# Transposing the next image in pairs of rows over four cycles, and averaging channel groups on VectorE by block transposes

## Chip, cores and metric

The kernel runs on one core of one Trainium2 chip. The time is that of one execution on the device, in microseconds (us), as the median of several executions. TensorE is the matmul engine (PE in the profile, PEld its weight loads), VectorE is DVE, ScalarE is ACT, GpSimd is POOL. L262 is line 262 of the kernel that is being spoken of.

## The reference

A batch of 32 images of 56 x 56 pixels and 128 channels, fp32, goes through two layers. Each is `x + layer(group_norm(x))` with 32 groups of 4 channels.

```python
# layer 0: shifted-window attention, 7 x 7 windows, 4 heads
x = x + attention(group_norm(x))
# layer 1: cosine transforms over width and over height, 32 modes mixed
# per mode by a 128 x 128 matrix, inverse transforms, then 128 -> 512 -> 128
x = x + feedforward(fourier(group_norm(x)))

def group_norm(v, G=32, eps=1e-5):          # v: B, H, W, C
    g = v.reshape(B, H, W, G, C // G)
    m, s = g.mean((1, 2, 4)), g.var((1, 2, 4))
    return (g - m) / sqrt(s + eps)
```

## The kernel before

An image is eight rows of windows. The kernel works in cycles, one per row: each cycle does the attention of one row of this image, in three stages on three rows, and a slice of the Fourier layer of the two images before. Behind an image's eighth cycle comes the first row of the next image, which must be ready by then: its pixels are transposed to channels on partitions (`image_group`), its statistics are gathered (`bn_stats`), and its group averages turn into the scale and shift of the first norm (`image_norm`). A generator's `yield` is where the cycle goes on with other work: `next(norm)` is called once behind the keys, once ahead of the second feed-forward matmul, and once at the cycle's end.

```python
    def image_group(im, i):                      # row i of windows: 3.5 tiles of 112 pixels
        pt = attn_bank()
        pt4 = pt[:, : 8 * S].rearrange("p (j r s) -> p j r s", r=8, s=WS)
        for c in range(4):                       # so every other tile is transposed twice
            nc.tensor.transpose(pt4[:, :, 2 * c : 2 * c + 2], im.x[:, WS * i // 2 + c], ...)
        mine = pt4[:, :, i % 2 : i % 2 + WS].rearrange("p j r s -> p j (r s)")
        ...
        nc.scalar.copy(xw.rearrange("p (j t) -> p j t", t=WT), mine)
        nc.vector.bn_stats(im.st[:, i], xw)
        ...
        nc.gpsimd.tensor_tensor(piece, piece, bproj..., ALU.add)     # the projection's bias

    def image_norm(im):
        mv = small.tile([P, 2], F32, tag="mv", name="mv")
        nc.vector.bn_aggr(mv, im.st)
        yield
        pg = attn_bank()                         # group mean: a block-diagonal matrix of 1/4
        nc.tensor.matmul(pg[:, 0:1], lhsT=gavg, rhs=mv[:, 0:1], start=True, stop=True)
        ...                                      # gm = mean; e = (mean_c - gm)^2 + var_c
        yield
        pv = attn_bank()                         # group variance
        nc.tensor.matmul(pv[:, 0:1], lhsT=gavg, rhs=e, start=True, stop=True)
        ...
        nc.gpsimd.tensor_tensor(rstd, ve, mhalf, ALU.pow)
        nc.vector.scalar_tensor_tensor(out=nb, in0=gm, scalar=-1.0, in1=rstd, ...)
        yield
        nc.scalar.mul(im.w, wqkv, rstd)
        pb = attn_bank()
        nc.tensor.matmul(pb[:, 0:1], lhsT=wqkv[:, 2 * C :], rhs=nb, start=True, stop=True)
        ...
    # in the cycle:
            for j in {4: (0, 1), 5: (2, 3, 4), 6: (5, 6, 7)}.get(i, ()):
                image_group(images[b + 1], j)
```

There is one `k_sb` and one `q_sb`; the keys are written twice, once by ScalarE and once by VectorE:

```python
    def attn_max(r):
        nc.vector.tensor_reduce(mx, a3, axis=AX.X, op=ALU.max)
        nc.gpsimd.tensor_tensor(a3, a3, mx..., ALU.subtract)
    def attn_exp(r):
        nc.scalar.activation(a3, a3, AF.Exp)
    def attn_qk(im, i, first):
        ...                                      # matmul into pq; ScalarE -> q
        ...                                      # matmul into pk; ScalarE -> k_sb[:, 0]
            nc.vector.tensor_scalar(k_sb[:, 1], pk3, ...)
    def full_last(cycle, norm):
        next(norm)
        ...                                      # second feed-forward matmul
        next_image(cycle)                        # transposes of the next image
        attn_exp(cycle)                          # ahead of the next cycle's keys
        attn_project(im, j)
        next(norm)
```

## Time and profile before

| | before |
|---|---|
| time, first 3 runs | 3686.11 us (3684.14 to 3687.61) |
| TensorE busy | 99% of the span, 61440 matmuls |
| VectorE, ScalarE, GpSimd busy | 59%, 58%, 37% |
| distance between the width transforms of two images, smallest of 29 | 112.51 us |
| the same, mean of 29 | 112.72 us |

The last two rows are the measure. They are read from TensorE's timeline: the start of one image's width cosine transform (L597, 112 matmuls) to the start of the next image's. All 32 images do the same work between those points, so the smallest distance is an image without irregular stops (I call it the floor) and the mean is what the time is made of. The first and last distances are left out, since they touch the start and the end.

### The profile page before, as it was taken

How to read it: one execution, taken by the hardware profiler on the slowest of the kernel's cores; microseconds unless marked ns; L12 is line 12 of the kernel's file. 1: busy time of each engine (PE TensorE's matmuls, PEld its weight loads, DVE VectorE, ACT ScalarE, POOL GpSimd, SP SyncE). 2: the span in 40 equal slices, each digit the busy share in tenths (PEclk: the TensorE clock that was granted, in tenths of full speed). 3: DMA queues.
4: the chain of work that ended last, by engine and by line, in shares of the span. 5: the costliest groups of instructions: out<-in, count | busy, mean ns of one | idle time of the engine just before them, and what ended most of it. 6: DMA issues, size and time to landing. Idle time of an engine off the chain costs nothing.

```text
span 3682.2 us, 139931 instructions
## 1 busy us (share of the span) xinstructions
PE 3627.3 (99%) x61440; PEld 2964.9 (81%) x61440; DVE 2184.9 (59%) x4580; ACT 2146.4 (58%) x3915; POOL 1370.7 (37%) x1421
## 2 busy tenths in 40 slices
PE   7899999999999999999999999999999999999999
PEld 5788888888888888888888888878888888888877
DVE  7656666556666556665566656566655566655641
ACT  5565555655556655566556565555565565665553
POOL 5333334333434333433334343334343333433321
PEclk9999999999999999999999999999999999999999
DMA  4334433433433334334334334343334343443333
GB/s 115 97 101 111 108 105 96 118 106 102 116 96 107 107 106 113 101 101 115 106 102 115 96 109 108 106 113 97 105 107 111 101 114 96 114 108 105 97 106 92
DMA packets 687792, 388.91 MB, mean 106 GB/s; under 512 B 40495, under 2 KB 658128, under 8 KB 686928
## 3 DMA queue, kind: packets, MB, share of 16 engines
q1 hardware_dynamic: 686573, 379.65, 37.7%
q8 instruction: 483, 7.91, 0.9%
q14 instruction: 125, 1.02, 0.1%
q10 hardware_dynamic: 611, 0.32, 0.0%
HBM read 218.29 MB, written 161.48 MB: 103 GB/s over the span
## 4 chain that ended last, share of the span: by engine, by line
PE 93%; DVE 4%; ACT 1%; DMA 1%; issue 0%; SPq 0%; POOL 0%; ACTq 0%; DVEq 0%; POOLq 0%
PE pc L733 20%; PE pc L713 18%; PE pa L355 7%; PE pc L631 6%; PE pc L597 6%; PE pa L377 5%; PE pa L421 5%; PE pa L488 5%; PE pa L330 5%; PE pc L670 5%; PE pa L446 4%; PE pa L323 4%; PE pa L261 2%; DVE a L385 1%; DVE st L272 1%; DVE mx L395 1%
## 5 line engine op out<-in xcount | busy, mean ns | idle before, releaser
L410 POOL TENSOR_TENSOR a<-a,rs 128x784 f32<-128x784 f32 x256 | 389.4, 1521 | 1218.7 <-DVE rs L409 958.7
L733 PE MATMUL pc<-wff,hid 128*128 128x128 f32 (+1 forms) x6400 | 778.8, 279 | 1.0 <-ACT hid L721 0.8
L733 PEld LDWEIGHTS pc<-wff,hid 128*128 128x128 f32 (+1 forms) x6400 | 731.4, 190 | 22.1 <-issue 2.9
L713 PE MATMUL pc<-xf,wff 128*128 128x512 f32 (+2 forms) x1792 | 713.4, 541 | 1.3 <-DVE xf L681 0.6
L721 ACT ACTIVATE hid<-pc,b1sb 128x512 f32<-128x512 f32 (+2 forms) x896 | 536.0, 635 | 93.3 <-PE pc L713 89.5
L713 PEld LDWEIGHTS pc<-xf,wff 128*128 128x128 f32 x1792 | 337.0, 190 | 302.6 <-issue 228.8
L396 POOL TENSOR_TENSOR a<-a,mx 128x784 f32<-128x784 f32 x256 | 389.2, 1520 | 462.3 <-DVE mx L395 451.1
L745 DVE TENSOR_TENSOR res<-pc,res 128x512 f32<-128x512 f32 (+3 forms) x259 | 143.8, 566 | 599.8 <-issue 282.0
L429 ACT COPY aT<-pa 113x452 f32<-113x452 f32 x256 | 137.3, 537 | 453.6 <-PE pa L421 453.5
L276 POOL TENSOR_TENSOR xl<-xl,bproj 112x384 f32<-112x384 f32 (+1 forms) x256 | 291.5, 1140 | 244.4 <-PE pa L261 240.3
L385 DVE TENSOR_TENSOR a<-pa,bm 128x392 f32<-128x392 f32 x512 | 259.7, 550 | 203.1 <-PE pa L377 202.9
L343 DVE TENSOR_SCALAR k<-pa,heads,bqkv 128x392 f32<-128x392 f32 x246 | 168.6, 685 | 279.3 <-ACT k L335 279.3
L402 ACT ACTIVATE a<-a 128x784 f32<-128x784 f32 x256 | 223.0, 871 | 182.6 <-POOL a L396 180.3
L477 DVE TENSOR_SCALAR oT<-pa,bqkv 128x98 f32<-128x98 f32 (+2 forms) x768 | 171.0, 279 | 259.3 <-PE pa L446 259.3
L362 ACT COPY v<-pa 128x512 f32<-128x512 f32 x256 | 152.5, 596 | 267.8 <-PE pa L355 267.6
L703 POOL TENSOR_TENSOR res<-res,b2sb 128x512 f32<-128x512 f32 (+2 forms) x256 | 263.2, 1034 | 96.2 <-DMA res<-scr 86.1
L377 PEld LDWEIGHTS pa<-k,q 64*64 64x64 f32 x8192 | 183.4, 132 | 128.3 <-DVE rs L409 68.2
L355 PE MATMUL pa<-wn,xw 128*64 128x128 f32 x4096 | 282.3, 280 | 3.6 <-DVE a L385 2.8
L355 PEld LDWEIGHTS pa<-wn,xw 128*64 128x64 f32 x4096 | 220.2, 137 | 53.5 <-issue 17.5
L395 DVE TENSOR_REDUCE mx<-a 128x16 f32<-128x784 f32 x256 | 247.4, 966 | 5.5
L421 PE MATMUL pa<-ident,a 113*113 113x113 f32 x2048 | 248.7, 265 | 0.9 <-POOL a L410 0.9
L407 DVE TENSOR_REDUCE sm<-a 128x16 f32<-128x784 f32 x256 | 245.9, 960 | 5.1 <-ACT a L402 5.1
(89 smaller groups left out, 5888.8 us busy)
## 6 DMA issues: line engine op xcount, KB each, us to landing
zscr<-z SPq DMA_DIRECT2D x512, 112.0 KB
htok<-scr SPq DMA_DIRECT2D x256, 196.0 KB
zT<-zscr SPq DMA_DIRECT2D x192, 256.0 KB
res<-scr SPq DMA_DIRECT2D x160, 256.0 KB
out_dram<-res SPq DMA_DIRECT2D x128, 256.0 KB
scr<-xl SPq DMA_DIRECT2D x128, 224.0 KB
xl<-in_x_dram SPq DMA_DIRECT2D x32, 784.0 KB
xl<-in_x_dram SPq DMA_DIRECT2D x32, 672.0 KB
```

What stands on the lines that cost most here:

```text
L276: nc.gpsimd.tensor_tensor(piece, piece, bproj.unsqueeze(1).to_broadcast([TC, n1 - n0, C]), ALU.add)
L355: nc.tensor.matmul(pv[hs, j * C : (j + 1) * C], lhsT=im.xw[i][:, w * WT : w * WT + JP], rhs=im.w[:, 2 * C : 3 * C], start=True, stop=True,)
L377: nc.tensor.matmul(ps[hp][HALVES[e], pr * 2 * WT : (pr + 1) * 2 * WT], lhsT=q[cs, w * WT : w * WT + JP], rhs=k_sb[cs, :, w], start=True, s ...
L385: nc.vector.tensor_tensor(a[:, 2 * hp : 2 * hp + 2, :, 0:WT].rearrange("p u w j -> p w u j"), ps[hp][:, :RT].rearrange("p (w u j) -> p w u ...
L395: nc.vector.tensor_reduce(mx, a3, axis=AX.X, op=ALU.max)
L396: nc.gpsimd.tensor_tensor(a3, a3, mx.unsqueeze(2).to_broadcast([P, 2 * NWR, WT]), ALU.subtract)
L410: nc.gpsimd.tensor_tensor(a3, a3, rs.unsqueeze(2).to_broadcast([P, 2 * NWR, WT]), ALU.mult)
L421: nc.tensor.transpose(pt[:PW, h * P : h * P + PW], a[:PW, h, 2 * hf : 2 * hf + 2].rearrange("p w j -> p (w j)")[:, :PW], ident[:PW, :PW],)
L703: nc.gpsimd.tensor_tensor(res[:m, c0:c1], res[:m, c0:c1], b2sb[:m].unsqueeze(1).to_broadcast([m, c1 - c0, C]), ALU.add,)
L713: nc.tensor.matmul(ph[:, :n], lhsT=wff1[:, f * P : (f + 1) * P], rhs=xff[:, t0 : t0 + n], start=True, stop=True,)
L721: nc.scalar.activation(hf[:, :n], ph[:, :n], AF.Relu, bias=b1sb[:, f : f + 1])
L733: nc.tensor.matmul(pf[:m, c * C : (c + 1) * C], lhsT=im.hid[f][:, c * P : c * P + m], rhs=wff2[:, f], start=(f == 0), stop=(f == NF - 1),)
```

## The change

The intent is to take matmuls from the engine that bounds the kernel. Two rows of windows are 7 whole tiles, so a pair needs 7 transposes where two single rows need 8; four pairs are spread over the fourth to seventh cycles. The two averaging matmul pairs go: VectorE transposes the 128 x 32 statistics within 32 x 32 blocks, so that a group of four channels lies along the free axis, reduces there, and transposes back. That chain stands behind the keys of the eighth cycle.

```diff
-    def image_group(im, i):
-        pt = attn_bank()
-        for c in range(4):
+    def image_groups(im, i):
+        pt = [attn_bank(), attn_bank()]
+        for c in range(7):
             nc.tensor.transpose(...)
-        nc.scalar.copy(xw.rearrange("p (j t) -> p j t", t=WT), mine)
-        nc.vector.bn_stats(im.st[:, i], xw)
+        for k in range(2):
+            ...                          # one copy for row 0, a small and a large one for row 1
+            nc.vector.bn_stats(im.st[:, i + k], xw)
...
     def image_norm(im):
-        nc.vector.bn_aggr(mv, im.st)
         yield
-        pg = attn_bank()
-        nc.tensor.matmul(pg[:, 0:1], lhsT=gavg, rhs=mv[:, 0:1], start=True, stop=True)
...
-        yield
-        pv = attn_bank()
-        nc.tensor.matmul(pv[:, 0:1], lhsT=gavg, rhs=e, start=True, stop=True)
+        nc.vector.bn_aggr(stat[:, 0:2], im.st)
+        nc.vector.transpose(turned, stat)
+        average(mean[:, 0], turned)      # tensor_reduce, then tensor_scalar by 0.25
+        nc.vector.tensor_tensor(turned, turned, mean[:, 0], ALU.subtract)
+        nc.vector.tensor_tensor(turned, turned, turned, ALU.mult)
+        average(mean[:, 1], turned)
+        nc.vector.transpose(back..., mean...)
...
         nc.gpsimd.tensor_tensor(rstd, ve, mhalf, ALU.pow)
+        yield
         nc.vector.scalar_tensor_tensor(out=nb, in0=gm, scalar=-1.0, in1=rstd, ...)
+        nc.scalar.mul(im.w, wqkv, rstd)
         yield
-        nc.scalar.mul(im.w, wqkv, rstd)
...
-            for j in {4: (0, 1), 5: (2, 3, 4), 6: (5, 6, 7)}.get(i, ()):
-                image_group(images[b + 1], j)
+            for j in {3: (0,), 4: (2,), 5: (4,), 6: (6,)}.get(i, ()):
+                image_groups(images[b + 1], j)
```

More of the change, by code (lines that the diff above doesn't have):

```diff
@@ L252, in image_begin @@
         return im
-    def image_group(im, i):
-        pt = attn_bank()
-        pt4 = pt[:, : 8 * S].rearrange("p (j r s) -> p j r s", r=8, s=WS)
-        for c in range(4):
+    def image_groups(im, i):
+        pt = [attn_bank(), attn_bank()]
+        pts = [
+            p[:, : n * S].rearrange("p (j r s) -> p j r s", r=n, s=WS) for p, n in zip(pt, (8, 6))
+        ]
+        for c in range(7):
             nc.tensor.transpose(
-                pt4[:, :, 2 * c : 2 * c + 2],
+                pts[c // 4][:, :, 2 * (c % 4) : 2 * (c % 4) + 2],
                 im.x[:, WS * i // 2 + c],
@@ L265, in image_group @@
             )
-        mine = pt4[:, :, i % 2 : i % 2 + WS].rearrange("p j r s -> p j (r s)")
-        im.xw[i] = big.tile([P, RT + JP - WT], F32, tag="xw", name="xw", bufs=10)
-        nc.gpsimd.memset(im.xw[i][:, RT:], 0.0)
-        xw = im.xw[i][:, :RT]
-        nc.scalar.copy(xw.rearrange("p (j t) -> p j t", t=WT), mine)
-        nc.vector.bn_stats(im.st[:, i], xw)
-        n0, n1 = WS * i // 2, WS * (i + 1) // 2
-        piece = im.x[:, n0:n1]
-        nc.gpsimd.tensor_tensor(
-            piece, piece, bproj.unsqueeze(1).to_broadcast([TC, n1 - n0, C]), ALU.add
-        )
@@ L280, in image_norm @@
-    def image_norm(im):
-        mv = small.tile([P, 2], F32, tag="mv", name="mv")
-        nc.vector.bn_aggr(mv, im.st)
-        yield
-        pg = attn_bank()
-        nc.tensor.matmul(pg[:, 0:1], lhsT=gavg, rhs=mv[:, 0:1], start=True, stop=True)
-        gm = small.tile([P, 1], F32, tag="gm", name="gm")
-        nc.vector.tensor_copy(gm, pg[:, 0:1])
+        for k in range(2):
+            im.xw[i + k] = big.tile([P, RT + JP - WT], F32, tag="xw", name="xw", bufs=10)
+            nc.gpsimd.memset(im.xw[i + k][:, RT:], 0.0)
+            xw = im.xw[i + k][:, :RT]
+            dst = xw.rearrange("p (j r s) -> p j r s", r=WS, s=WS)
+            if k:
+                nc.scalar.copy(dst[:, :, 0], pts[0][:, :, WS])
+                nc.scalar.copy(
+                    dst[:, :, 1:].rearrange("p j r s -> p j (r s)"),
+                    pts[1].rearrange("p j r s -> p j (r s)"),
+                )
+            else:
+                nc.scalar.copy(
+                    dst.rearrange("p j r s -> p j (r s)"),
+                    pts[0][:, :, :WS].rearrange("p j r s -> p j (r s)"),
+                )
+            nc.vector.bn_stats(im.st[:, i + k], xw)
@@ new lines, in image_groups, with image_norm, average @@
+        n0, n1 = WS * i // 2, WS * (i + 2) // 2
+        for a, e in ((n0, n0 + 4), (n0 + 4, n1)):
+            piece = im.x[:, a:e]
+            nc.gpsimd.tensor_tensor(
+                piece, piece, bproj.unsqueeze(1).to_broadcast([TC, e - a, C]), ALU.add
+            )
+    stat = const.tile([P, C // 4], F32, tag="stat", name="stat")
+    nc.vector.memset(stat, 0.0)
+    def image_norm(im):
+        GR = C // 16
+        def average(out, src):
+            sums = small.tile([P, GR], F32, tag="gsums", name="gsums", bufs=2)
+            nc.vector.tensor_reduce(
+                sums, src.rearrange("p (g c) -> p g c", c=4), axis=AX.X, op=ALU.add
+            )
+            nc.vector.tensor_scalar(
+                out.rearrange("p (g c) -> p g c", c=4),
+                sums.unsqueeze(2).to_broadcast([P, GR, 4]),
+                0.25,
+                None,
+                ALU.mult,
+            )
+        yield
+        nc.vector.bn_aggr(stat[:, 0:2], im.st)
+        turned = small.tile([P, 32], F32, tag="turned", name="turned", bufs=2)
+        nc.vector.transpose(turned, stat)
+        mean = small.tile([P, 2, 32], F32, tag="gmeans", name="gmeans", bufs=2)
+        average(mean[:, 0], turned)
+        nc.vector.tensor_tensor(turned, turned, mean[:, 0], ALU.subtract)
+        nc.vector.tensor_tensor(turned, turned, turned, ALU.mult)
+        average(mean[:, 1], turned)
+        back = small.tile([P, 2, 32], F32, tag="back", name="back", bufs=2)
+        nc.vector.transpose(
+            back.rearrange("p k c -> p (k c)"), mean.rearrange("p k c -> p (k c)")
+        )
+        gm = back[:, 0, 0:1]
@@ L290, in image_norm @@
         nc.vector.tensor_scalar(im.xw[0][:, RT : RT + 1], gm, -1.0, None, ALU.mult)
-        d = small.tile([P, 1], F32, tag="d", name="d")
-        nc.vector.tensor_tensor(d, mv[:, 0:1], gm, ALU.subtract)
-        e = small.tile([P, 1], F32, tag="e", name="e")
+        ve = small.tile([P, 1], F32, tag="ve", name="ve")
         nc.vector.scalar_tensor_tensor(
-            out=e, in0=d, scalar=d, in1=mv[:, 1:2], op0=ALU.mult, op1=ALU.add
+            out=ve, in0=back[:, 0, 1:2], scalar=1e-5, in1=back[:, 1, 0:1], op0=ALU.add, op1=ALU.add
@@ L296, in image_norm @@
         )
-        yield
-        pv = attn_bank()
-        nc.tensor.matmul(pv[:, 0:1], lhsT=gavg, rhs=e, start=True, stop=True)
-        ve = small.tile([P, 1], F32, tag="ve", name="ve")
-        nc.vector.tensor_scalar(ve, pv[:, 0:1], 1e-5, None, ALU.add)
         rstd = small.tile([P, 1], F32, tag="rstd0", name="rstd0")
         nc.gpsimd.tensor_tensor(rstd, ve, mhalf, ALU.pow)
+        im.w = work.tile([P, 3 * C], F32, tag="wn", name="wn")
+        yield
         nb = small.tile([P, 1], F32, tag="nb0", name="nb0")
@@ L307, in image_norm @@
         )
-        im.w = work.tile([P, 3 * C], F32, tag="wn", name="wn")
+        nc.scalar.mul(im.w, wqkv, rstd)
         yield
-        nc.scalar.mul(im.w, wqkv, rstd)
         pb = attn_bank()
@@ L923, in swin_fourier_kernel @@
         images[0] = image_begin(0)
-        for i in range(NWR):
-            image_group(images[0], i)
+        for i in range(0, NWR, 2):
+            image_groups(images[0], i)
         for _ in image_norm(images[0]):
```

## The prediction

> **What bounds the kernel now.** I read the busy table first, then the chain that ended last, then TensorE's timeline over one image, then the other engines over the same stretch, then the table of waits.
>
> ```profile
> PE 3627.3 (99%) x61440; PEld 2964.9 (81%) x61440; DVE 2184.9 (59%) x4580; ACT 2146.4 (58%) x3915; POOL 1370.7 (37%) x1421
> PEclk9999999999999999999999999999999999999999
> ...
> PE 93%; DVE 4%; ACT 1%; DMA 1%; issue 0%; SPq 0%; POOL 0%; ACTq 0%; DVEq 0%; POOLq 0%
> ```
>
> TensorE is busy in 99% of the span, its clock is granted in full, and 93% of the chain is TensorE. So what counts is TensorE time taken out, less the new waits of TensorE. But its busy rows can't be added up: ends are modelled, and the means of the groups (273 ns for a transpose, 263 and 216 ns for the averaging matmuls) are latencies of which most overlaps the next matmul. The cost on the path is the distance from the start of one burst to the start of the next, read from the timeline. These rows are from the cycles of one image that the change touches (fifth to eighth row of windows; the next image is transposed at their ends):
>
> ```profile
> 1703.94 0.98 PE L261 MATMUL pa<-ident_x,xl 112*128 112x112 f32 x8
> 1704.76 0.82 PE L488 MATMUL pa<-wproj,oT 128*112 128x128 f32 x6
> ...
> 1712.99 0.81 PE L446 MATMUL pa<-aT,v 49*32 49x49 f32 x64
> 1713.73 1.49 PE L261 MATMUL pa<-ident_x,xl 112*128 112x112 f32 x12
> 1715.06 1.04 PE L488 MATMUL pa<-wproj,oT 128*112 128x128 f32 x8
> 1715.93 0.96 PE L421 MATMUL pa<-ident,a 113*113 113x113 f32 x8
> 1716.72 0.84 PE L323 MATMUL pa<-xw,wn 128*128 128x392 f32 x2
> 1717.64 0.93 PE L330 MATMUL pa<-xw,wn 128*128 128x392 f32 x2
> 1718.40 2.32 PE L713 MATMUL pc<-xf,wff 128*128 128x320 f32 x8
> ...
> 1729.53 1.44 PE L261 MATMUL pa<-ident_x,xl 112*128 112x112 f32 x12
> 1730.81 0.82 PE L488 MATMUL pa<-wproj,oT 128*112 128x128 f32 x6
> ...
> 1733.59 0.28 PE L286 MATMUL pa<-mv,gavg 128*128 128x1 f32 x2
> 1733.73 1.97 PE L713 MATMUL pc<-xf,wff 128*128 128x256 f32 x8
> ...
> 1741.12 0.38 PE L299 MATMUL pa<-e,gavg 128*128 128x1 f32 x2
> 1741.37 2.03 PE L733 MATMUL pc<-wff,hid 128*128 128x128 f32 x16
> ```
>
> The columns are start, duration, group. Transposes take 0.82, 1.33 and 1.28 us for 8, 12 and 12, so 3.43 us an image, 107 ns each. The first averaging matmul costs 0.14 us (1733.59 to 1733.73), the second 0.25 us. One thing more is hidden in these rows: from L323 to L330 it is 0.92 us in the sixth cycle, and 0.67 us in the others (1706.21 to 1706.88). L330 waits there, and the wait table says for what:
>
> ```profile
> PEld pa L330 <- DVE xl L496: 33.0, 88, 0.7
> DVE nb L305 <- POOL rstd L303: 22.9, 32, 2.1
> ```
>
> L330 writes the bank that the projection left, and VectorE empties that (L496) only after its three bn_stats of the transposed rows (1715.50 to 1716.91, L496 until 1717.59). From the width DCT of one image to that of the next the undisturbed distance is 112.52 us; nearly all of the span is 32 of these plus the start and the end.
>
> **What the Trainium skill says.** "Perfetto Trace Analysis", section "Identifying the Most-Contended Engine", warns that matmul busy time is a poor measure because matmuls are pipelined; the trace agrees (12.4 us busy in 64 matmuls of L299, 0.25 us on the path for each pair). "TensorE: Matmul & The Clock Gate", section "LDWEIGHTS (loading the stationary operand)", gives the number of columns over 1.2 as ns, 107 ns for 128; a transpose holds the image as 128 columns of weights, and the 107 ns apart agree. "VectorE: DVE Perf Modes", section "The three transpose paths", says that VectorE transposes within 32x32 blocks only, which is enough here, as groups of four channels lie inside a block; no such instruction is in this trace. "GPSIMD Engine Reference", section "1. Specifications", says GpSimd shares its SBUF interfaces with VectorE instructions that have two SBUF inputs. The trace agrees: L305, of two SBUF inputs, takes 0.16 us alone and 1.22 us wherever GpSimd's L703 has just started, ending with it.
>
> **The change part by part.**
> Transposes: four pairs of rows take 7 tiles each, at the ends of cycles four to seven, in place of 0, 8, 12 and 12. At 102 to 107 ns a pair costs about 0.72 us. The fourth cycle gains +0.72, the fifth -0.10 (0.82 to 0.72), the seventh -0.56 (1.28 to 0.72). The sixth is special: nothing but transposes lies between the attention-values matmuls and the projection, whose input VectorE and ScalarE evacuate. In the last image, with no next one, the projection there starts 1.87 us after the values; so with 7 transposes (done at 0.74 + 0.72 = 1.46) it waits till 1.87 rather than 2.07 now: -0.20. One bn_stats less (0.47 us apart) brings L496 to about 4.13 us after the values, so L330 starts at 1.87 + 1.67 + 0.67 = 4.21 and no longer waits: a further -0.24, and -0.10 for the next group, which after the wait took 0.76 instead of 0.66. Together +0.72 - 0.10 - 0.54 - 0.56 = -0.48 us an image.
> Averages: both matmul pairs go, -0.14 and -0.25, -0.39 us. The third (L312) stays.
> VectorE in the eighth cycle: eleven small instructions after the keys in place of four there and one before. At 0.15 to 0.22 us, plus 34 ns between dependent ones (1.1 us of idle in 32), the aggregate at 0.36 and the wider reductions and transposes estimated at 0.2, the chain is about 2.5 us against 0.6 now, so what follows is some 1.9 us later. There VectorE has slack: it idles 1.91 us before the oT evacuations at 1741.26, and what consumes the exponential is in the next cycle. GpSimd stands idle in the chain, since the power is queued ahead of its next work, so no port is shared.
> ScalarE: three copies for two, the small one about 0.2 us, 0.8 us an image at 58% load. In a pair's cycle the second row is ready about 1.7 us after the transposes begin, its bn_stats ends at 2.3, L496 at about 2.8 (three tiles) or 2.9 (four), and L330 would come at 2.84 or 3.05: level, so no large wait.
> Loads: the fourth cycle needs the image 14 us earlier. Its load was issued at 1671.0 us, the traffic of it ends near 1681, and the transposes would come at 1689.5: 8 us to spare. The DMA queue's order of instructions is the same in both programs.
> Sum: -0.48 - 0.39 = -0.87 us an image. It applies to 30 of 32; the first is transposed alone and the second in the start, where VectorE and not TensorE leads. That is -26 us. In four or five images the sixth cycle's projection already waits for ScalarE, held by a transfer, and gains nothing there (-2 us of gain). In the start the chain of averages meets GpSimd's bias additions, which reach to 19.0 us, where the power starts today anyway: 0 to +2 us.
>
> **The rivals.**
> (a) Busy time counts in full: 128 transposes at 126 ns (129.2 us over 1024), 16 us, and 21.8 us of averaging with 5 us of idle: 43 us, giving 3643. Against it stands the start-to-start reading; I give it 5%.
> (b) A wait takes the place of the one removed: `nb` (L305 now) moves ahead of the eighth cycle's expansion, behind the oT evacuations at about 9.05 us after L330 starts. By then GpSimd runs the subtraction of the maxima (8.4 to 9.95) and right after it L703 (to 11.2). Having two SBUF inputs, `nb` ends at about 10 if it slips in between, else at 11.2, and TensorE wants it at 10.8. The second would cost 0.4 to 0.55 us an image, 12 to 16 us: 3672 to 3676. At the start one such instruction got through between two additions, and copies beside memsets did not, so I give it 40%.
> (c) The averaging chain is longer than estimated: from about 2.8 us on, the score evacuation (L385), whose bank the values matmuls reuse, holds TensorE; each 0.3 us more costs 9 us. 20%.
> (d) The fourth cycle waits for the load or for the other engines: 8 us of spare speaks against it. 5%.
> (e) The gain is swallowed because VectorE is the real bound in the pair cycles: the level race of L496 and L330 could cost 0.1 us in three cycles, 9 us. 25%.
>
> **Range and chances.** The plain sum gives 3686.1 - 26 + 2 + 1 = 3663; half of (b)'s weight and some of (e) take back 5 us, the slack found elsewhere (the 0.10 us at L421 in the eighth cycle) may return 2: I say 3665. With everything well it is about 3652, with (b) and (c) or (e) together about 3678. Over 2% would be 74 us, beyond even rival (a); a loss of 2% would need a wait of over 3 us an image, which nothing shows.
>
> **What would show each step right or wrong.** Right: the PE row counts 61184 matmuls (128 transposes and 128 averaging ones fewer); the distance between width DCTs falls from 112.5 to 111.5 to 111.9 us; in the sixth cycle the projection follows the values by 1.87 us and L323 to L330 is 0.67 us; the transposes of a pair take 0.7 to 0.75 us; VectorE's chain lasts 2.2 to 2.8 us. Rival (b) shows as waits of TensorE for `nb`, of 0.3 us or more, in most images, with `nb` over 1 us long; (c) as the values matmuls waiting for `a`; (d) as transposes waiting for the image; (e) as L330's successor waiting for the projection's sum in three cycles of each image. Wrong altogether I would be if the distance fell by over 1.2 us or by less than 0.3.

## The result

| | before | after |
|---|---|---|
| time, median of 6 runs | 3687.51 us (3684.14 to 3688.34) | 3666.47 us (3664.53 to 3671.09) |
| ratio, 95% interval | | 0.9947 (0.9934 to 0.9960): within 2% |
| floor of the distance between width transforms | 112.51 us | 111.93 us |
| its mean over 29 images | 112.72 us | 112.23 us |

A ratio, here and below, is the mean time of one kernel's fast runs over the mean of the other's fast runs of the same rounds, so it is not quite the ratio of the medians. It puts the change at 3687.51 x 0.0053 = 20 us. The predicted time was 3665.

The profiled execution of the changed kernel happens to be its slowest (3671.09); its matmul count and its chain are these:

```profile
PE 3603.8 (98%) x61184; PEld 2938.0 (80%) x61184; DVE 2222.3 (61%) x4741; ACT 2152.8 (59%) x4043; POOL 1371.9 (37%) x1421
...
PE 91%; DVE 4%; ACT 2%; POOL 1%; issue 1%; DMA 0%; SPq 0%; POOLq 0%; DVEq 0%; ACTq 0%
```

The 256 matmuls are gone. Less of the chain is TensorE (91% for 93%), and more of it ScalarE and GpSimd (2% and 1% for 1% and 0%). Where, one sixth cycle shows. This is TensorE's timeline of the changed kernel, start and duration in us, then line and tiles; L482 is the values, L262 the transposes, L524 the projection, L359 and L366 queries and keys, L749 the first feed-forward matmul, L413 the scores (before: L446, L261, L488, L323, L330, L713, L377):

```profile
1594.65 0.81 PE L482 MATMUL pa<-aT,v 49*32 49x49 f32 x64
1595.39 0.99 PE L262 MATMUL pa<-ident_x,xl 112*128 112x112 f32 x7
1596.52 1.10 PE L524 MATMUL pa<-wproj,oT 128*112 128x128 f32 x8
1597.45 0.95 PE L457 MATMUL pa<-ident,a 113*113 113x113 f32 x8
1598.24 0.84 PE L359 MATMUL pa<-xw,wn 128*128 128x392 f32 x2
1598.92 0.84 PE L366 MATMUL pa<-xw,wn 128*128 128x392 f32 x2
1599.60 2.32 PE L749 MATMUL pc<-xf,wff 128*128 128x320 f32 x8
1602.07 0.91 PE L413 MATMUL pa<-k,q 64*64 64x98 f32 x32 [0.15 <-DVE k L379]
```

The prediction shows the same cycle of the kernel before, from 1712.99 on. The row that follows there is this one:

```profile
1720.65 0.90 PE L377 MATMUL pa<-k,q 64*64 64x98 f32 x32
```

Counted from the start of the values, the projection comes at 1.87 us for 2.07, L366 follows L359 by 0.68 for 0.92, and the feed-forward matmul starts at 4.95 for 5.41: 0.46 us is won so far, of the 0.54 predicted. But the scores start at 7.42 us for 7.66. Half of the gain is lost in front of them, at a wait for the keys (`DVE k L379`) that the kernel before does not have there.

Over all 29 steady images, the median distance from each burst of matmuls to the next gives where the floor's 0.58 us comes from:

| at the end of cycle | what | before | after | difference | predicted |
|---|---|---|---|---|---|
| 4th | transposes | 0 | 0.708 | +0.708 | +0.72 |
| 5th | transposes | 0.820 | 0.717 | -0.103 | -0.10 |
| 6th | transposes to projection | 1.334 | 1.130 | -0.204 | -0.20 |
| 6th | projection to the next | 0.874 | 0.935 | +0.061 | 0 |
| 6th, then | queries to keys | 0.915 | 0.673 | -0.242 | -0.24 |
| 6th, then | keys to feed-forward | 0.762 | 0.680 | -0.082 | -0.10 |
| 6th, then | feed-forward to scores | 2.247 | 2.466 | **+0.219** | 0 |
| 6th, then | the inverse transform | | | +0.018 | 0 |
| 7th | transposes | 1.281 | 0.761 | -0.520 | -0.56 |
| 7th, then | first averaging pair and the feed-forward matmul behind it | 0.140 + 1.903 | 1.820 | -0.223 | -0.14 |
| in the 8th | second averaging pair and the feed-forward matmul behind it | 0.244 + 1.868 | 1.888 | -0.224 | -0.25 |
| | sum | | | -0.592 | -0.87 |

("Then" marks rows that are already the beginning of the next cycle; I go on calling them the sixth cycle's, as the prediction does.)

The profiled executions differ by 3682.2 - 3669.3 = 12.9 us. By parts: the first width transform comes 1.7 us later, the second image is 2.7 us shorter, the 29 steady ones 14.3 us shorter (16.9 by the floor, 2.6 given back to irregular stops), and the end is 2.3 us longer. The start scatters: in the four kernels whose start is nearly the change's own (experiments 3, 7, 8 and 9) the first width transform comes anywhere from 106.1 to 109.2 us (106.3 before, 108.1 after the change). And this is the slowest run of its six, so the difference of these two executions is smaller than that of the medians.

**The new wait.** The keys of the next cycle wait for a row of instructions over three engines. VectorE, GpSimd and ScalarE of the changed kernel in the same cycle:

```profile
1596.29 0.96 DVE L431 TENSOR_REDUCE mx<-a 128x16 f32<-128x784 f32 x1
...
1601.33 0.69 DVE L379 TENSOR_SCALAR k<-pa,heads,bqkv 128x392 f32<-128x392 f32 x1 [1.42 <-ACT k L371]
```

```profile
1597.39 1.52 POOL L432 TENSOR_TENSOR a<-a,mx 128x784 f32<-128x784 f32 x1 [3.30 <-DVE mx L431]
```

```profile
1598.94 0.87 ACT L438 ACTIVATE a<-a 128x784 f32<-128x784 f32 x1 [1.96 <-POOL a L432]
...
1600.61 0.68 ACT L371 ACTIVATE k<-pa,bqkv,heads 128x392 f32<-128x392 f32 x1
```

Row maxima end at 1597.25, GpSimd's subtraction starts at 1597.39 and ends at 1598.91, the exponential (L438) starts at 1598.94. Behind it in ScalarE's order stand a copy of the weights `aT`, the queries and the keys, and behind those VectorE's half of the keys, which ends at 1602.02; the scores start at 1602.07. Nothing in this row waits for the matmuls of the keys, which had ended by 1599.8. It hangs on the evacuation of the scores before. In the kernel before, VectorE's half of the keys ends equally late:

```profile
1719.66 0.69 DVE L343 TENSOR_SCALAR k<-pa,heads,bqkv 128x392 f32<-128x392 f32 x1 [0.95 <-ACT k L335]
```

That is 7.36 us after the start of the values (1712.99), for 7.37 after the change. Before, TensorE came 0.3 us later than that and did not notice.

**The averaging chain** in the eighth cycle, on VectorE, some of its rows and what follows it:

```profile
1616.08 0.36 DVE L316 BATCH_NORM_AGGREGATE stat<-st 128x2 f32<-128x48 f32 x1
1616.48 0.21 DVE L319 STREAM_TRANSPOSE turned<-stat 128x32 f32<-128x32 f32 x1
...
1618.40 0.15 DVE L334 SCALAR_TENSOR_TENSOR ve<-back 128x1 f32<-128x1 f32 x1
...
1620.09 0.97 DVE L421 TENSOR_TENSOR a<-pa,bm 128x392 f32<-128x392 f32 x2
...
1622.57 1.19 DVE L342 SCALAR_TENSOR_TENSOR nb<-back,rstd 128x1 f32<-128x1 f32 x1
```

It lasts from 1616.08 to 1618.55, 2.47 us. The row of the evacuation of the scores (L421) is two instructions, one for each bank: by the single records the first ends at 1620.60, the second at 1621.07, and the values matmuls start at 1621.08. The values need the bank of the first (experiment 7), so there is slack of somewhat under half a microsecond here. On GpSimd, at the same time:

```profile
1622.21 1.52 POOL L432 TENSOR_TENSOR a<-a,mx 128x784 f32<-128x784 f32 x1 [0.37 <-DVE mx L431]
1623.69 1.28 POOL L739 TENSOR_TENSOR res<-res,b2sb 128x512 f32<-128x512 f32 x1
```

`nb` is one column, and lasts 1.19 us. It starts while L432 runs and ends at 1623.76, just after L432 ends at 1623.73; it slips in ahead of L739. TensorE wants it at 1624.58. The Trainium skill says why, in "SBUF — State Buffer", section "Who interferes with whom": a VectorE instruction with two SBUF inputs contends with a GpSimd instruction that reads SBUF, and whichever has the shared interface keeps it for its whole instruction while the other is blocked. The trace agrees: in 29 of the 32 images `nb` ends 0.01 to 0.02 us after L432.

### The profile page after: what moved, and what is told of

Same layout as the page of the kernel before. It is cut to its first block, busy times and chain, and to the rows that moved or that the text cites. A ratio compares the mean times of both kernels' runs of the same rounds, so it can differ in the third digit from the quotient of the medians.

```text
span 3669.3 us, 139900 instructions
## 1 busy us (share of the span) xinstructions
PE 3603.8 (98%) x61184; PEld 2938.0 (80%) x61184; DVE 2222.3 (61%) x4741; ACT 2152.8 (59%) x4043; POOL 1371.9 (37%) x1421
## 4 chain that ended last, share of the span: by engine, by line
PE 91%; DVE 4%; ACT 2%; POOL 1%; issue 1%; DMA 0%; SPq 0%; POOLq 0%; DVEq 0%; ACTq 0%
PE pc L769 21%; PE pc L749 17%; PE pa L391 7%; PE pc L667 6%; PE pc L633 6%; PE pa L413 6%; PE pa L457 5%; PE pc L706 5%; PE pa L524 5%; PE pa L482 4%; PE pa L359 4%; PE pa L366 4%; PE pa L262 2%; POOL a L432 1%; DVE a L421 1%; DVE mx L431 1%
## 5 line engine op out<-in xcount | busy, mean ns | idle before, releaser
L446 POOL TENSOR_TENSOR a<-a,rs 128x784 f32<-128x784 f32 x256 | 389.6, 1522 | 993.0 <-DVE rs L445 869.7
L749 PE MATMUL pc<-xf,wff 128*128 128x512 f32 (+2 forms) x1792 | 710.9, 539 | 0.9 <-DVE xf L717 0.6
L749 PEld LDWEIGHTS pc<-xf,wff 128*128 128x128 f32 x1792 | 339.5, 190 | 310.3 <-issue 229.4
L432 POOL TENSOR_TENSOR a<-a,mx 128x784 f32<-128x784 f32 x256 | 388.8, 1519 | 456.9 <-DVE mx L431 448.0
L289 POOL TENSOR_TENSOR xl<-xl,bproj 112x512 f32<-112x512 f32 (+1 forms) x256 | 286.0, 1138 | 347.3 <-PE pa L262 338.8
L421 DVE TENSOR_TENSOR a<-pa,bm 128x392 f32<-128x392 f32 x512 | 259.7, 550 | 203.2 <-PE pa L413 203.1
L438 ACT ACTIVATE a<-a 128x784 f32<-128x784 f32 x256 | 225.0, 879 | 222.3 <-POOL a L432 221.9
L379 DVE TENSOR_SCALAR k<-pa,heads,bqkv 128x392 f32<-128x392 f32 x246 | 168.6, 685 | 288.0 <-ACT k L371 288.0
L739 POOL TENSOR_TENSOR res<-res,b2sb 128x512 f32<-128x512 f32 (+2 forms) x256 | 263.7, 1035 | 98.5 <-DMA res<-scr 88.3
L413 PEld LDWEIGHTS pa<-k,q 64*64 64x64 f32 x8192 | 183.6, 132 | 137.7 <-DVE rs L445 67.5
L524 PE MATMUL pa<-wproj,oT 128*112 128x128 f32 x1792 | 241.0, 274 | 12.6 <-DVE oT L513 7.2
```

Of the source, the lines that this page charges most:

```text
L289: nc.gpsimd.tensor_tensor(piece, piece, bproj.unsqueeze(1).to_broadcast([TC, e - a, C]), ALU.add)
L413: nc.tensor.matmul(ps[hp][HALVES[e], pr * 2 * WT : (pr + 1) * 2 * WT], lhsT=q[cs, w * WT : w * WT + JP], rhs=k_sb[cs, :, w], start=True, s ...
L421: nc.vector.tensor_tensor(a[:, 2 * hp : 2 * hp + 2, :, 0:WT].rearrange("p u w j -> p w u j"), ps[hp][:, :RT].rearrange("p (w u j) -> p w u ...
L432: nc.gpsimd.tensor_tensor(a3, a3, mx.unsqueeze(2).to_broadcast([P, 2 * NWR, WT]), ALU.subtract)
L446: nc.gpsimd.tensor_tensor(a3, a3, rs.unsqueeze(2).to_broadcast([P, 2 * NWR, WT]), ALU.mult)
L524: nc.tensor.matmul(pp[:TC, (n - n0) * C : (n - n0 + 1) * C], lhsT=oT[:, (n - base) * TC : (n - base + 1) * TC], rhs=wproj, start=True, sto ...
```

## The experiments

Ten kernels ran, all correct. Medians are not compared between batches, as the kernel before itself had medians of 3690.09 (22 runs), 3690.66 (9) and 3689.19 us (8) in the three batches; the ratios are to those. One microsecond is 0.00027.

**1. The pairs alone** (the old averages kept):

```diff
-            for j in {4: (0, 1), 5: (2, 3, 4), 6: (5, 6, 7)}.get(i, ()):
-                image_group(images[b + 1], j)
+            for j in {3: (0,), 4: (2,), 5: (4,), 6: (6,)}.get(i, ()):
+                image_groups(images[b + 1], j)
```

> The transposes in pairs with the old averages. Theory A (the gain is the distance between burst starts, less a wait for the keys in the sixth cycle): the pairs bring 0.71 - 0.10 - 0.25 - 0.52 = -0.16 us an image in the 29 steady distances, so about 5 us less than before (0 to 9). Theory B (what I predicted: no wait takes the sixth cycle's gain): -0.48 us an image, 14 us less. Rival (busy time counts in full, 128 x 126 ns): 16 us less.

Measured: 3686.45 us (16 runs), ratio 0.9987 (0.9980 to 0.9995), 4.8 us; floor 112.39 us, 0.12 less than before. The 0.48 us that I had predicted for this part is refuted, and so is the busy time. The wait for the keys is in this run too (feed-forward to scores 2.466 us, median), so it comes from the pairs and not from the averages.

**2. The averages alone** (single rows kept):

```diff
-        pg = attn_bank()
-        nc.tensor.matmul(pg[:, 0:1], lhsT=gavg, rhs=mv[:, 0:1], start=True, stop=True)
+        nc.vector.transpose(turned, stat)
+        average(mean[:, 0], turned)
... (as in the change)
```

> The new averages with the old four transposes for each row. Theory A, from the two traces: the first averaging pair costs 0.22 us with what it does to the next burst, the second 0.22, so -0.45 us an image, 13 us less than before (9 to 17), and together with the pairs alone the sum of the whole change. As predicted (0.14 + 0.25 = 0.39): 12 us, not told apart. Rival (busy time and idle in full): 27 us less.

Measured: 3679.43 us (7 runs), ratio 0.9971 (0.9960 to 0.9981), 10.7 us; floor 112.05 us, 0.46 less than before. By the floors the averages give about four fifths of the gain, and the two parts add up: 0.12 + 0.46 = 0.58, that of the whole. By the ratios they come to 4.8 + 10.7 = 15.5 of 20 us; each of the three ratios is uncertain by 3 to 5 us, so this is not a contradiction, but not a confirmation either.

**3. The sixth cycle's exponential behind the next cycle's keys.** If the row of instructions described above is what holds the scores, the exponential (0.87 us of ScalarE) need only leave it:

```diff
     def full_first(cycle, norm):
...
         im, i = row(cycle)
         if im:
             attn_qk(im, i, False)
+        late = (cycle - 1) % NWR == 5 and row(cycle - 1)[0]
+        if late:
+            attn_exp(cycle - 1)
...
-        if row(cycle)[0]:
+        if row(cycle)[0] and cycle % NWR != 5:
             attn_exp(cycle)
```

(The squares of the second norm also go behind the division there, to keep the order of ScalarE and VectorE free of a mutual wait.)

> The whole change, but the exponential of the sixth cycle stands behind the query and key evacuations of the next cycle, not ahead of them. Theory A (there the scores wait for the keys, and these stand on ScalarE behind an exponential that waits for GpSimd): the burst from L749 to the scores falls back from 2.47 to 2.25 us, 0.2 us an image, 6 us faster than the change (3 to 8), if no bank waits for the hidden layer's evacuation instead. Rival (the keys are late because VectorE is): the wait stays, within 2 us of the change.

Measured: 3665.74 us (5 runs), ratio 0.9929 (0.9916 to 0.9941); floor 111.69 us, 0.24 less than the change. The scores follow the feed-forward matmul by its own length again:

```profile
1600.60 2.32 PE L749 MATMUL pc<-xf,wff 128*128 128x320 f32 x8
1602.84 0.90 PE L413 MATMUL pa<-k,q 64*64 64x98 f32 x32
```

That is 2.24 us (median of the images 2.247) for 2.466. The theory of the keys is confirmed: the wait is gone with what was said to cause it. By the ratios the gain over the change is 6.6 us, by the floor 0.24 us an image, about 7 us. What is shown is the wait and the floor. For the time it is less sure: the intervals of the two ratios overlap, and in the profiled execution irregular stops took the gain back (mean distance 112.21 us for 112.23).

**4. Half of the sixth cycle's mode mixing between the values and the transposes.** TensorE waits for the projection's input and for the keys in that cycle; matmuls that need neither could fill the wait.

```diff
-                for g in range(4):
+                for g in range(2):
                     mix(im, False, g)
+    def late_mix(cycle):          # called after the values
+        for im, c in fourier(cycle):
+            if c == 3:
+                for g in range(2, 4):
+                    mix(im, False, g)
```

> The whole change, but half of the mode-mixing matmuls of the sixth cycle (1.8 us) stand between the attention values and the transposes. Theory A: TensorE then has work while the attention output is evacuated, so the projection's wait there (1.13 us from the transposes' start to it, against 0.71) and the wait for the keys go: 0.41 + 0.06 + 0.22 = about 0.7 us an image, 20 us faster than the change (12 to 21). Rival: the later half of the mixing delays its trip through DRAM, and the inverse transform of the next cycle waits for it: no gain or a loss, seen as waits of L706's successor for zT.

Measured: 3671.46 us (5 runs), ratio 0.9948 (0.9935 to 0.9962), no gain; floor 111.40 us, but mean 112.38. Half of the theory was right: an undisturbed image is 0.53 us shorter (the matmuls that were split in two bursts cost 0.15 us more than in one, 1.847 + 1.899 for 3.594). Few images are undisturbed, since the modes mixed later go through a buffer in DRAM and the seventh cycle's inverse transform wants them:

```profile
PE pc L706 <- DMA zT<-zscr: 13.3, 17, 2.0
```

13.3 us in 17 waits of TensorE, where the change has one. The rival, a transfer that was hidden and is no longer, was right about the time.

**5. The same, with the inverse transform behind its cycle's own mixing, and four buffers instead of three for mixed modes.**

```diff
+    def back(cycle, which):       # the seventh cycle's call moves behind half_columns
-            for width, g in back_groups(c):
-                modes_back(im, width, g)
+            if which(c):
+                for width, g in back_groups(c):
+                    modes_back(im, width, g)
```

> The split mixing once more, with the height's inverse transform of the seventh cycle put behind that cycle's mixing (2.8 us later) and a fourth z buffer. In the split mixing alone the steady distance fell to 111.40 us at its best, as theory A has it, but in 13 of 29 images TensorE stood before the inverse transform (L413 to L706 up to 2.40 us in place of 0.73). If the trip through DRAM was the cause, these waits go, the distances lie within 0.3 us of 111.4, and the kernel is 12 to 22 us faster than the change, 31 to 41 faster than before. If the cause was ScalarE or the banks, the wait only moves with it and the kernel stays within 5 us of the change.

Measured: 3660.66 us (4 runs), ratio 0.9919 (0.9904 to 0.9934); floor 111.60, mean 112.00 us; of the 17 waits of TensorE for `zT` two are left (2.3 us). About 10 us faster than the change by the ratios (0.0028 x 3688), a little less than expected.

**6. The same with three buffers**, to see whether the order alone does it (`bufs=4` back to `bufs=3`):

> The kernel with half of the mode mixing moved ahead and the inverse transform moved behind its cycle's mixing, with three instead of four buffers for the mixed modes. It asks whether the fourth buffer was needed for the gain or the order alone. Theory A (the order alone): the smallest distance between width transforms 111.6 us and the mean near 112.0 as with four buffers, no wait of the inverse transform for its transfer, ratio to before .990 to .9935. Rival B (buffers): a wait of the mixing's evacuation for a free buffer shows, and the mean distance is 0.2 to 0.5 us longer (6 to 15 us in all), ratio .9935 to .996.

Measured: 3659.41 us (4 runs), ratio 0.9923 (0.9906 to 0.9939); floor 111.60, mean 112.08 us. The order alone is enough. Versions 5 and 6 are the fastest found; their intervals do not tell them apart.

**7. A longer chain.** Two more averages, whose results are overwritten with the same values, probe how much slack there is behind the chain.

```diff
         average(mean[:, 1], turned)
+        for _ in range(2):
+            average(mean[:, 1], turned)
```

> The whole change with two more group averages, done again for nothing, so the chain on VectorE behind the keys takes 3.33 in place of 2.47 us. Theory A (the slack before the attention values of the eighth cycle is 0.4 us by the trace: score evacuation done at 1620.64, values at 1621.08): the other 0.45 us hold TensorE in each image, 13 us slower than the change (9 to 18). Rival (the chain lies wholly beside TensorE's work): within 3 us of the change.

Measured: 3678.81 us (6 runs), ratio 0.9968 (0.9957 to 0.9980), 7.7 us slower than the change (the intervals just overlap); floor 112.10, 0.17 more. I expected more, because I took an added average for 0.4 us. In the trace the chain grew by 0.60 us for both (3.07 for 2.47), since an average that does not wait for the one before overlaps it. In the eighth cycle the step from the values to the next burst grew from 0.738 to 0.902 us: in 29 images the third weight load of the values now starts 0.05 us after the first of the two score evacuations ends. So 0.60 - 0.16 = 0.44 us was slack, and a chain over about 2.9 us holds TensorE. The change is below that limit by half a microsecond, not by much.

**8. The chain ahead of the keys** (at the end of the seventh cycle):

```diff
     def image_norm(im):
-        yield
         nc.vector.bn_aggr(stat[:, 0:2], im.st)
...
         im.w = work.tile([P, 3 * C], F32, tag="wn", name="wn")
         yield
+        yield
```

> The whole change with the chain issued at the end of the seventh cycle, ahead of the attention copies and the keys, in place of behind the keys. Theory A: VectorE gets to its half of the keys some 2 us later, and the scores, now 0.15 us or so behind the keys, wait about 1.5 us in each image: 35 to 52 us slower than the change. Rival (the place of a 2.5 us chain on an engine 61% busy does not matter): within 5 us of it.

Measured: 3713.67 us (4 runs), ratio 1.0066 (1.0049 to 1.0083), slower than the kernel before; floor 113.27 us, 1.34 more than the change. TensorE's waits have at their head:

```profile
PE pa L413 <- DVE k L379: 41.3, 44, 1.5
```

(us in all, times, longest.) The place behind the keys is worth twice the whole gain of the change (44 us by the ratios, against 20).

**9. `nb` with one tensor input.** Rival (b) of the prediction feared that `nb`, lengthened by GpSimd, would hold TensorE. The same product with `rstd` as a per-partition scalar has one SBUF tensor input:

```diff
-        nc.vector.scalar_tensor_tensor(
-            out=nb, in0=gm, scalar=-1.0, in1=rstd, op0=ALU.mult, op1=ALU.mult
-        )
+        nc.vector.tensor_scalar(nb, gm, rstd, -1.0, ALU.mult, ALU.mult)
```

> The whole change with nb computed by an instruction with one tensor input and the reciprocal root as a scalar from memory, not by one with two tensor inputs. If the port shared with GpSimd makes nb take 1.18 us: it falls to 0.15 to 0.3 us. Theory A says that TensorE does not wait for nb (it is done 0.8 us before it is wanted), so the time stays within 3 us of the change. Rival b of the prediction (nb holds TensorE): 10 us or more faster.

The group of `nb` in the changed kernel, and then in this one (busy us, mean ns of one):

```profile
L342 DVE SCALAR_TENSOR_TENSOR nb<-back,rstd 128x1 f32<-128x1 f32 x32 | 34.8, 1089 | 0.7 <-POOL rstd L338 0.7
```

```profile
L342 DVE TENSOR_SCALAR nb<-back,rstd 128x1 f32<-128x1 f32 x32 | 6.5, 204 | 0.7 <-POOL rstd L338 0.7
```

1089 ns become 204, and the floor stays at 111.93 us: TensorE did not wait for it. The time, 3674.94 us (4 runs), ratio 0.9957 (0.9942 to 0.9973), is that of the change within its interval. This kernel's profiled execution had more irregular stops than most (mean distance 112.60); whether they are also what its four runs (3670.20 to 3679.05) scatter by is not shown, as the others have no trace.

**10. The first image's bias additions behind its norm.** In the start the chain lasts 5.2 us, not 2.5. GpSimd adds the projection's bias to the image at that time. Put those additions later:

```diff
-            image_groups(images[0], i)
+            image_groups(images[0], i, False)      # without the bias
...
+        for i in range(0, NWR, 2):
+            image_bias(images[0], i)               # after image_norm
```

> The changed kernel, with the first image's eight bias additions on GpSimd put after that image's first norm instead of before it. In the changed kernel the averaging chain takes 5.2 us at the start and 2.5 us in every later image. If the running bias additions stretch the two-input VectorE instructions of the chain there, the first chain should now take about 2.5 us (2.4 to 2.8), with L322 and L323 near 0.2 us each. Theory A: the start is bound by the first keys and by the bias table, which is ready only some us later, so the time moves by no more than 1 us (ratio to before .994 to .9955, as the change's .9947), and the time from the start to the first image's width transform moves by under 1 us. Rival B: the chain's 2.7 us come off the start in full, and the first width transform starts 2.5 to 3 us earlier.

Measured: 3672.35 us (5 runs), ratio 0.9961 (0.9948 to 0.9974), so about 5 us slower than the change by the ratios, whose intervals overlap, and the first width transform 3.1 us later (at 111.2 us; in the eleven other kernels 103.2 to 109.2). Neither theory. VectorE in the start of the changed kernel, and of this one:

```profile
15.26 0.92 DVE L322 TENSOR_TENSOR turned<-turned,gmeans 128x32 f32<-128x32 f32 x1
...
21.88 5.70 DVE L182 TENSOR_TENSOR bm<-rpb,mask 49x98 f32<-49x98 f32 x32 [1.05 <-DMA rpb<-rpb_cols]
```

```profile
15.58 0.19 DVE L326 TENSOR_TENSOR turned<-turned,gmeans 128x32 f32<-128x32 f32 x1
...
22.15 9.43 DVE L182 TENSOR_TENSOR bm<-rpb,mask 49x98 f32<-49x98 f32 x32 [2.24 <-DMA rpb<-rpb_cols]
```

The chain is 2.6 us, as expected (0.19 for 0.92 us in this instruction). Not only instructions of two inputs had been stretched: the chain's multiplication by 0.25 (L307), with one SBUF tensor, took 0.50 and 0.69 us beside the additions and takes 0.18 without them. But the additions then ran from 17.7 to 26.5 us, beside the building of the attention bias table, 32 VectorE additions of two SBUF inputs each: 9.43 us for 5.70. The first scores are evacuated 4.0 us later, 0.03 us after the table's end in both kernels; in all eleven other kernels that happens between 27.6 and 28.6 us, here at 31.6. What blocked the chain now blocks the table, which sits on the path of the start while the chain did not. I had checked what the additions would leave, and not what they would meet.

## Why the prediction was right, and where it was wrong

The number held: 3665 against 3666.47, well inside the range. By its own steps:

- **Start-to-start distances instead of busy time: right.** Busy time would have given 43 us; the time moved by 20.
- **Transposes of a pair at 0.70 to 0.75 us: right** in the fourth and fifth cycle (0.708, 0.717), and nearly in the seventh (0.761).
- **The sixth cycle: wrong by 0.31 us**, and this is the step that failed. "The projection at 1.87 after the values" and "L330 no longer waits" came exactly so (1.87; 0.673 us). But the cycle did not get shorter by that much: 0.22 us went into a wait for the keys and 0.06 into a slower projection. I followed the matmuls to the one behind the wait that I removed, and stopped there; the next input of TensorE with a fixed time, the keys at 7.37 us, was 0.3 us away. No rival named it. Experiment 3 shows it.
- **Averages: 0.39 predicted, 0.46 measured** (experiment 2, whose 10.7 us are the expected 12 within the interval). The first pair cost more than its distance of 0.14 us: the burst behind it was longer too, 1.903 for 1.820.
- **Chain of 2.5 us: right** (2.46 to 2.47 in each steady image). Rival (c) did not come, but its mechanism, with the limit "from about 2.8 us on", was right: experiment 7 shows the values waiting for the score evacuation from about 2.9 us on. The reading of the place behind the keys is confirmed by experiment 8.
- **Rival (b)**, which had 40%: `nb` took over a microsecond, as feared, but it slipped in between the two GpSimd instructions. It did not hold TensorE (experiment 9).
- **Rivals (d), (e) and (a)**: no wait for the image; L366 at 0.673 us after L359 in the pairs' cycles, so TensorE lost nothing to the race there. (The weight loads of L366 still wait for L532, 119 times in the wait table for 88 before, 0.3 us each, but while the matmul ahead of them runs.)
- **The start**: no loss of 0 to 2 us can be told from its scatter; the second image gained 2.7 us in the profiled execution, which I had not counted.

So the time was nearer than the working deserves. The sum of 0.87 us in 30 images was 26 us; measured by the floor it is 0.58, or 17 (the time moved by 20). The correction of 5 us for rivals that then did not come, and the loss of 3 us for irregular images and the start, stand by chance where the wait for the keys should have stood.

**What stays open.** TensorE stops for about 1 us within a burst in some images, with no releaser in the profile ("issue"), as here in the changed kernel:

```profile
2558.87 2.61 PE L633 MATMUL pc<-dct_w,xl 112*64 112x64 f32 x83
2562.47 1.09 PE L633 MATMUL pc<-dct_w,xl 112*64 112x64 f32 x29 [0.99 <-issue]
```

In the profiled execution of the kernel before, the distances exceed the floor by 6.0 us in all; after the change by 8.6, in experiment 3 by 15.0, in 5 by 11.5 (in 4, with its waits for transfers, by 28.4). Only a part of this excess has no releaser: 4.2 us of TensorE's idle time before, 6.8 after, 8.4 in experiment 3. It is tempting to say that a wait removed is given back to these stops, but in experiment 7, where a wait was added, they are 8.5 us. With one execution of each kernel no such rule is shown, and what the stops are no run here tells.

## What to carry to other kernels

When a wait on the bounding engine is removed, go on along that engine to the next input whose time is set by something else, and count the gain only up to there; here the keys had 0.3 us of slack and took the rest. Splitting a change in two runs and comparing the floor of a repeated distance, not the total, showed within a few hundredths of a microsecond which part had not paid. Before moving GpSimd work, list the VectorE instructions it will newly run beside, those of two SBUF inputs first: taken off a chain that had slack, it cost more on the table that had none.

## What the Trainium skill lacked or had wrong

- "GPSIMD Engine Reference", section "1. Specifications", and "SBUF — State Buffer", section "Who interferes with whom", name the VectorE instructions that contend with GpSimd, but not what this costs small ones. Here a one-column VectorE instruction took 1.18 us beside GpSimd's subtraction of 1.52 us and 0.16 us alone, a chain of eleven took 5.2 us instead of 2.5 beside additions of 1.0 to 1.3 us each, and 32 additions took 9.43 instead of 5.70.
- "VectorE: DVE Perf Modes", section "The three transpose paths", has one VectorE duration, for bf16 128 x 128 (311 ns). In fp32, 128 x 32 took 0.21 us and 128 x 64 took 0.245 us in these runs.
- "VectorE: DVE Perf Modes", section "Rules for kernel authors", says that a reduction along the partition axis is not possible on VectorE. For groups within a block of 32 partitions it is, by a block transpose, a reduction and a transpose back: mean and variance together took 2.47 us here, and every run agreed with the reference.
- No page that I read covers stops of TensorE of about 1 us within a dense burst, without a releaser in the profile (0.99 us in the row above).
